# Factors of differences on GpSimd and ACT, units of two kinds in turn, experts chosen by sequence: a change to the last attention of an eight-layer kernel

## The chip, the core and the metric

The kernel runs on one core of one Trainium2 chip. The metric is the device time of one execution, in microseconds (us). The profile is one execution taken by the hardware profiler; its engines are PE (TensorE, matrix products), DVE (VectorE), ACT (ScalarE), POOL (GpSimd) and SP (the queue that starts most transfers). PE reads its operands from SBUF and writes into PSUM[...]. Each engine runs its instructions in the order in which they were queued, and waits for others by semaphores.

## The reference

The program is four pairs of an attention and a feed-forward, each followed by a residual sum and a layer norm, on x of 8 sequences, 256 positions and 256 features. Only the last pair is changed:

```python
# L3_attn: 16 heads of 16 features, each with two query/key pairs (a = 0, 1)
energy = einsum('bqhad,bkhad->bahqk', rope(q), rope(k)); causal mask
scores = softmax(energy / sqrt(16))
lam    = exp(sum(lq1*lk1)) - exp(sum(lq2*lk2)) + 0.2          # one per head
diff   = softmax(where(causal, NEG, scores[:, 0] - lam * scores[:, 1]))
att    = einsum('bhqv,bvhd->bqhd', diff, v); rms norm of each head; @ Wo
# L3_ffn: 32 experts, the 4 best of each token
probs  = softmax(x @ gate); w, idx = top_k(probs, 4); w = w / w.sum()
y      = sum over the 4 experts of w * ((u * silu(g)) @ down),  g, u = x @ gate_up
```

The softmax of a difference of two softmaxes is the heart of it: for each row, with e0 and e1 the exponentials of the two scores and s0, s1 their sums, the kernel forms e0 + c * e1 with c = -lam * s0 / s1 and scales it by r = 1 / s0. The ratio of the weights of the four experts does not depend on the sum over all 32.

## The kernel before, in words

Everything is one program written in a tile language; in the last attention and the last feed-forward the order of the instructions is written out by hand, and each engine keeps it.

**The attention (`attn3`).** The work is cut into 48 units, six for each sequence b. A unit has a half of the queries (qc) and some heads for four slots s: with qc = 0 it has two heads per slot and 128 keys (first kind: `Unit(b, 0, 0)` and `Unit(b, 0, 2)`), with qc = 1 one head and 256 keys (second kind: `Unit(b, 1, 0..3)`). Both kinds have the same number of scores, in four PSUM banks (tags "a" and "s", two buffers each); the first kind has sixteen exponentials of 128 elements, the second eight of 256. The order is by sequence, first the two units of the first kind, then the four of the second.

The loop over n at the end of `attn3` is a pipeline over units. Iteration n queues:
- `factors` of unit n-1: reciprocal r of the sums (L671, DVE), selection of the causal part of e0 with a fill (L676, POOL, two halves), c = s0 * r1 (L681) and c times minus lambda (L682), both POOL;
- `scores` of unit n: products (L641) and mask (L654) on PE, four negative maxima (L658, DVE), exponentials with their sums (L661, ACT);
- `values` of unit n-3: products with V (L738), and for the last head group a copy to oS (L118 or L120);
- a step of the projection of the next sequence (L595 on PE, evicted at L599 by DVE);
- the first half (slots 0 and 1) of `differences` of unit n-1: c * e1 + e0 (L695, DVE, one instruction for each slot and head), its negative maximum (L699, DVE), that times r (L700, POOL), and v = r * d + maximum (L703, POOL);
- one or two more steps of the projection, and a step of `finish` of an earlier sequence (L755 to L803: transposes, head norm, output product, residual, layer norm, and the transposed x for the feed-forward at L154);
- the second half of `differences`, then steps of the queue `others`;
- `turned` of unit n-2: v transposed by PE (L720) in two halves, each followed by an exponential on ACT (L722).

Projection, `finish`, `turned` and the gate products below all use PSUM banks of the tag "t", of which there are two.

**The experts (`ffn3_sort`, `place`, `scatter`).** The sequences form two groups of four. When x of sequence 3 is done, `others` gets the sort of group 0 for all eight tiles of 128 tokens at once: gate products (L1906), softmax over the experts without its sum (L1911 to L1916), the eight largest and their indices (L1921, L1922), then `place`: which expert has how many tokens (L893 to L902), where its tile begins, a slot for each token and expert (L907 to L926), and `tile_experts` (L935 to L944). Then 32 indirect transfers of POOL write the tokens to their slots in HBM (L953), three for each unit.

**The feed-forward (`ffn3`).** SP fetches the sorted rows in tiles (L1959) after the scatter is complete, then starts the loads of the down weights (L132). `ffn3_experts` goes over 63 tiles of group 0: transposes (L1970), products with gate and up (L1978), silu (L1985, ACT), product (L1987, DVE), transpose back (L1994), down (L2000), and a store. One small POOL copy per tile (L1990) marks the steps. Beside these tiles run what is left of `finish`, and then `ffn3_sort` for group 1. Then come the 63 tiles of group 1 with `ffn3_combine` of group 0 beside them (gathers L2045, weighted sums L2051), and at the end `ffn3_combine` of group 1.

Of the kernel before, what the change touches and what calls it, by code (L numbers as in the profile page):

```python
# [18 lines left out]
P = 128  # L19
# [20 lines left out]
class Model:  # L40


    def __init__(self, ctx, tc, ins, out):
# [23 lines left out]
        self.scattering = False  # L67
# [42 lines left out]
    def after(self, *call):  # L110

        self.left.append(call)

# [438 lines left out]
    def attn3(self, w, act, keep, start=False, beside=None):  # L552
# [4 lines left out]

        nc = self.nc
# [66 lines left out]
        class Unit:  # L625
# [41 lines left out]
            def factors(u):  # L667

                g = nc.gpsimd
                u.r = self.small.tile([P, 4, u.nh, 2], F32, tag="r3", name="r3")  # L670
                nc.vector.reciprocal(u.r, u.sums)  # L671
                u.c = self.small.tile([P, 4, u.nh], F32, tag="c3", name="c3")

                for i in range(2):
                    diag = u.e[:, 2 * i : 2 * i + 2, :, 0, u.nk - P :]
                    g.affine_select(  # L676
                        diag, diag, pattern=[[0, 2], [0, u.nh], [-1, P]],
                        compare_op=ALU.is_ge, fill=NEG, base=0, channel_multiplier=1,
                    )
                    if i == 0:  # L680
                        g.tensor_tensor(u.c, u.sums[:, :, :, 0], u.r[:, :, :, 1], ALU.mult)  # L681
                        g.tensor_tensor(  # L682
                            u.c, u.c, nlam[:, :, u.h0 : u.h0 + u.nh], ALU.mult
                        )

            def differences(u):
# [4 lines left out]
                for i in range(2):  # L691
                    two = slice(2 * i, 2 * i + 2)
                    for s in (2 * i, 2 * i + 1):
                        for h in range(u.nh):
                            nc.vector.scalar_tensor_tensor(  # L695
                                d[:, s, h, :], u.e[:, s, h, 1, :], u.c[:, s, h : h + 1],
                                d[:, s, h, :], ALU.mult, ALU.add,
                            )
                    nc.vector.tensor_reduce(nm[:, two], d[:, two], AX.X, ALU.max, negate=True)  # L699
                    nc.gpsimd.tensor_tensor(nm[:, two], nm[:, two], u.r[:, two, :, 0], ALU.mult)  # L700
                    for s in (2 * i, 2 * i + 1):
                        for h in range(u.nh):
                            nc.gpsimd.tensor_scalar(  # L703
                                u.v[:, s, h, :], d[:, s, h, :], u.r[:, s, h, 0:1],
                                nm[:, s, h : h + 1], ALU.mult, ALU.add,
                            )
                    yield
# [40 lines left out]
        def finish(b):  # L748
# [64 lines left out]
            if beside and b == GROUPS[0][1] - 1:  # L813
                others.append(beside(keep))
            yield

        others = []
        projections, ends, done = [], [], []

        def step(queue, n=1):  # L820

            while n and queue:
                if next(queue[0], StopIteration) is StopIteration:
                    queue.pop(0)
                else:
                    n -= 1

        for _ in project(0):
            pass
        units = [  # L830
            Unit(b, qc, h0) for b in range(NB) for qc in range(2) for h0 in range(0, 4, 2 - qc)
        ]
        for n in range(len(units) + 3):
# [11 lines left out]
            step(others)  # L845
# [11 lines left out]
            if not self.scattering:  # L857
                step(others, 2)
# [4 lines left out]
        return ends + others  # L863
# [1031 lines left out]
    def ffn3_sort(self, w, g, act, each=1):  # L1895


# [5 lines left out]
        lg = self.ps("t")[:, : n * 32].rearrange("p (t e) -> p t e", e=32)  # L1903
        for t in range(n):
            for c in range(2):
                nc.tensor.matmul(  # L1906
                    lg[:, t, :], self.xt(first + t // 2, t % 2, c), w["gate"][:, c, :],
                    start=(c == 0), stop=(c == 1),
                )
        nm = act.tile([P, n], F32, tag="r_nm", name="r_nm", bufs=1)  # L1910
        nc.vector.tensor_reduce(nm, lg, AX.X, ALU.max)  # L1911
        pr = act.tile([P, n, 32], F32, tag="r_pr", name="r_pr", bufs=1)
        nc.vector.tensor_tensor(
            pr, lg, nm.unsqueeze(2).to_broadcast([P, n, 32]), ALU.subtract
        )
        nc.scalar.activation(pr, pr, AF.Exp)  # L1916
        yield
        top = act.tile([P, n, 8], F32, tag="r_top", name="r_top", bufs=1)
        idx = act.tile([P, n, 8], U32, tag="r_idx", name="r_idx", bufs=1)
        for t in range(n):  # L1920
            nc.vector.max(top[:, t, :], pr[:, t, :])  # L1921
            nc.vector.max_index(idx[:, t, :], top[:, t, :], pr[:, t, :])  # L1922
            if t % 4 == 3 or t == n - 1:
                yield
        one, slots, ends = yield from self.place(w, act, self.const, f"f3{g}", idx[:, :, 0:4], n)
# [3 lines left out]
        next(rows)  # L1929
        expert = yield from self.tile_experts(w, act, self.const, f"f3{g}", ends)  # L1930

        wt = self.const.tile([P, n, 4], F32, tag=f"r_w{g}", name="r_w", bufs=1)
        sm = act.tile([P, n], F32, tag="r_sm", name="r_sm", bufs=1)
        nc.vector.tensor_reduce(sm, top[:, :, 0:4], AX.X, ALU.add)
        nc.vector.reciprocal(sm, sm)
        nc.vector.tensor_tensor(
            wt, top[:, :, 0:4], sm.unsqueeze(2).to_broadcast([P, n, 4]), ALU.mult
        )
        self.sorted[g] = wt, slots, expert
        self.scattering = True  # L1940
        yield
        for i, _ in enumerate(rows):
            if i % each == each - 1:
                yield
        self.scattering = False

    def ffn3_experts(self, w, g, act):
# [3 lines left out]
        rows, outs, expert, tiles = self.rows[g], self.outs[g], self.sorted[g][2], TILES[g]  # L1951
# [77 lines left out]
    def ffn3_combine(self, g, act, ahead):  # L2029
# [4 lines left out]
        wt, slots, _ = self.sorted[g]  # L2034
# [28 lines left out]
    def ffn3(self, w, act, left, start=False):  # L2063
# [3 lines left out]
        self.down = None  # L2067
        if start:
            for b in range(NB):
                self.transpose_x(b)  # L2070
            left = [self.ffn3_sort(w, 0, act)]
        if 0 not in self.sorted:
            for x in left:
                for _ in x:
                    pass
            left = []
        left = list(left) + [self.ffn3_sort(w, 1, act)]
        for j, _ in enumerate(self.ffn3_experts(w, 0, act)):

            if len(left) > 1 and j % 3 != 2:  # L2080
                continue
            while left and next(left[0], StopIteration) is StopIteration:
                left.pop(0)
        for x in left:
            for _ in x:
                pass
        put = self.ffn3_combine(0, act, 2)
# [6 lines left out]
        for _ in self.ffn3_combine(1, act, 1):  # L2094
            pass
# [3 lines left out]
def tile_layers(ctx: ExitStack, tc: tile.TileContext, ins, out, phases):  # L2099
# [26 lines left out]
    for i, name in enumerate(phases):  # L2126
        m.last = i == len(phases) - 1
        with tc.tile_pool(name=f"act{i}", bufs=2, side=sides[i % 2]) as act:
# [4 lines left out]
            with tc.manual_schedule(engines=engines) if name in MANUAL else ExitStack():  # L2133
# [20 lines left out]
                elif name == "attn3":  # L2154
                    beside = None
                    if not m.last:
                        beside = partial(m.ffn3_sort, stack[i + 1][1], 0, each=3)
                    left = m.attn3(w, act, kept[i], start=start, beside=beside)
                elif name == "ffn3":
                    m.ffn3(w, act, left, start=start)  # L2160
                    keeps[i - 1].close()
# [128 lines left out]
```

## Time and profile before

| what | us |
|---|---|
| median of three runs (2530.45 to 2537.91) | 2533.2 |
| the profiled execution's own time | 2531.46 |
| its span, from the first to the last instruction | 2529.7 |
| PE busy in the span | 2207.9 |
| DVE busy | 1431.1 |
| ACT busy | 1046.2 |
| POOL busy | 917.4 |
| last attention: first exponential to last | 1770.8 to 2225.5 |
| last feed-forward: first fetch of rows | 2226.92 |

Of each engine the profile counts the time in which an instruction is at work, not the time in which it waits. A share over the whole span says little here, since the eight layers have different limits; the stage between 1770 and 2226 us, and what follows it, has to be read by itself. In the timeline a row gives the start, the time it took, the engine, the line of the kernel and what was written and read; in brackets stands how long the engine had been idle before, and what ended that. Rows that follow each other without a gap are merged, so that "x2" means two instructions.

### The profile page before, as it was taken

Reading aid. Unit: us, or ns where it says so; the run is one execution under the profiler, and the core shown is the slowest. Engines: PE = TensorE matmul, PEld = TensorE weight load, DVE = VectorE, ACT = ScalarE, POOL = GpSimd, SP = SyncE. Lnnn points to the kernel's source line nnn. Section 1 sums busy time; section 2 is a strip of 40 time slices with the busy share of each in tenths; the row PEclk is TensorE's granted clock in tenths of the full one; section 3 lists DMA queues with packets and bytes.
Section 4 is the critical chain, followed back from the end, with each engine's and each line's share of the span. In section 5 each row is a group of like instructions: output and inputs, shape, how many; then the busy total and the mean of one; then the engine's idle time right before and its main releaser. Section 6 shows DMA issues by size and latency. Waiting matters only on the chain. (4 is left out here: it accounts for less than half of the span.)

```text
span 2529.7 us, 36310 instructions
## 1 busy us (share of the span) xinstructions
PE 2207.9 (87%) x12016; PEld 1497.5 (59%) x12016; DVE 1431.1 (57%) x3593; ACT 1046.2 (41%) x3005; POOL 917.4 (36%) x1725
## 2 busy tenths in 40 slices
PE   7999789899999999999999999998878777678990
PEld 4454588756666666666664465555555554467780
DVE  4555486754544544544465454565888888645363
ACT  1334355553544544534431112121766755634440
POOL 1222443343433323333312321000566647824445
PEclk9999999999999999999999999999989988789995
DMA  5000411100000100000250011002000000155663
GB/s 159 1 1 1 157 48 40 53 14 4 4 3 3 52 1 1 1 1 1 81 197 0 1 50 51 1 0 102 1 2 1 1 1 28 38 139 174 200 203 96
DMA packets 92309, 120.76 MB, mean 48 GB/s; under 512 B 9757, under 2 KB 79582, under 8 KB 91102
## 3 DMA queue, kind: packets, MB, share of 16 engines
q1 hardware_dynamic: 82270, 95.75, 11.8%
q0 software_dynamic: 8192, 21.11, 2.8%
q8 instruction: 100, 1.64, 0.3%
q10 hardware_dynamic: 1664, 1.57, 0.2%
q14 instruction: 83, 0.68, 0.1%
HBM read 67.53 MB, written 50.88 MB: 47 GB/s over the span
## 5 line engine op out<-in xcount | busy, mean ns | idle before, releaser
L1388 POOL TENSOR_SCALAR p<-p,rs 128x128 f32<-128x128 f32 (+1 forms) x256 | 104.6, 428 | 293.7 <-DVE rs L1386 289.4
L1378 ACT ACTIVATE p<-ps_s,nm,rq 128x128 f32<-128x128 f32 (+1 forms) x256 | 128.0, 507 | 151.0 <-DVE nm L1376 151.0
L1306 ACT ACTIVATE sq<-ps_a 128x512 f32<-128x512 f32 x126 | 76.0, 603 | 228.1 <-PE ps_a L1298 225.9
L146 POOL TENSOR_SCALAR rsq<-bnmv 128x2 f32<-128x2 f32 x64 | 13.6, 213 | 385.4 <-DVE bnmv L184 377.8
L661 ACT ACTIVATE e<-ps_a,nm 128x128 f32<-128x128 f32 (+1 forms) x256 | 105.9, 435 | 108.9 <-DVE nm L658 95.4
L1307 DVE TENSOR_REDUCE ssk<-sq 128x4 f32<-128x512 f32 x64 | 43.8, 686 | 172.6 <-ACT sq L1306 172.6
L703 POOL TENSOR_SCALAR v<-e,r,nmd 128x128 f32<-128x128 f32 (+1 forms) x256 | 134.9, 540 | 10.0
L1298 PE MATMUL ps_a<-w_a_wq,xT 128*128 128x512 f32 x256 | 123.2, 604 | 12.1 <-DVE k L1320 9.2
L1978 PE MATMUL ps_a<-w_f_gup,xTg 128*128 x504 | 113.1, 349 | 12.8 <-DVE xTg L1972 5.5
L720 PE MATMUL ps_t<-ident,v 128*128 128x128 f32 x384 | 67.8, 312 | 62.3 <-DVE qT L599 30.6
L1298 PE MATMUL ps_a<-w_a_wv,xT 128*128 128x512 f32 x256 | 120.5, 593 | 1.0 <-ACT q L1331 1.0
L695 DVE SCALAR_TENSOR_TENSOR e<-e,c 128x128 f32<-128x128 f32 (+1 forms) x256 | 105.6, 462 | 23.0 <-POOL c L682 22.8
L1307 DVE TENSOR_REDUCE ssq<-sq 128x4 f32<-128x512 f32 x64 | 43.9, 686 | 131.0 <-ACT sq L1306 131.0
L1298 PE MATMUL ps_a<-w_a_wk,xT 128*128 128x512 f32 x248 | 116.5, 593 | 0.0
L1426 PE MATMUL ps_o<-w_a_wo,attT 128*128 128x256 f32 x512 | 111.8, 379 | 0.0
L661 ACT ACTIVATE e<-ps_s,nm 128x128 f32<-128x128 f32 (+1 forms) x256 | 106.8, 451 | 0.0
L1426 PEld LDWEIGHTS ps_o<-w_a_wo,attT 128*128 128x128 f32 x512 | 96.7, 190 | 12.8
L1162 DVE SCALAR_TENSOR_TENSOR yg<-ps_t,xg,yg 128x128 f32<-128x128 f32 x266 | 93.1, 350 | 13.8 <-PE ps_t L1151 3.5
L1365 PE MATMUL ps_s<-kT,qT 128*128 128x256 f32 (+1 forms) x512 | 99.5, 327 | 0.0
L1978 PEld LDWEIGHTS ps_a<-w_f_gup,xTg 128*128 128x128 f32 x504 | 83.3, 199 | 25.2 <-issue 10.5
L720 PEld LDWEIGHTS ps_t<-ident,v 128*128 128x128 f32 x384 | 49.4, 160 | 81.8 <-POOL nmd L700 29.9
L1412 PE MATMUL ps_o<-pT,V 128*128 128x256 f32 x256 | 79.5, 392 | 19.3 <-ACT pT L120 19.3
(410 smaller groups left out, 6072.7 us busy)
## 6 DMA issues: line engine op xcount, KB each, us to landing
rows<-zero SPq DMA_DIRECT2D x42, 384.0 KB
xg<-rows SPq DMA_DIRECT2D x42, 384.0 KB
outs<-yg SPq DMA_DIRECT2D x42, 384.0 KB
w_f_gup<-in_f_gup SPq DMA_DIRECT2D x8, 768.0 KB
w_f_w<-in_f_w SPq DMA_DIRECT2D x8, 512.0 KB
w_f_down<-in_f_down SPq DMA_DIRECT2D x8, 384.0 KB
w_f_up<-in_f_up SPq DMA_DIRECT2D x5, 512.0 KB
lrows<-zero SPq DMA_DIRECT2D x12, 204.0 KB
```

Source lines behind the costliest of these rows:

```text
L661: nc.scalar.activation(e[:, s, j * nk : (j + 1) * nk], sc[s][:, j, :], AF.Exp, bias=nm[:, s, j : j + 1], scale=1.0, accum_out=sums[:, s, j ...
L695: nc.vector.scalar_tensor_tensor(d[:, s, h, :], u.e[:, s, h, 1, :], u.c[:, s, h : h + 1], d[:, s, h, :], ALU.mult, ALU.add,)
L703: nc.gpsimd.tensor_scalar(u.v[:, s, h, :], d[:, s, h, :], u.r[:, s, h, 0:1], nm[:, s, h : h + 1], ALU.mult, ALU.add,)
L720: nc.tensor.transpose(ps[:, s, c, :], x, self.ident)
L1162: nc.vector.scalar_tensor_tensor(acc[j], y, c, acc[j], ALU.mult, ALU.add)
L1298: nc.tensor.matmul(ps, self.xt(u.b, t, c), w[which][:, c, u.cols], start=(c == 0), stop=(c == 1),)
L1307: nc.vector.tensor_reduce(out, sq, AX.X, ALU.add)
L1365: nc.tensor.matmul(sc[:, j, :], u.qT[:, h0 + j, qc * P : (qc + 1) * P], u.kT[:, h0 + j, 0:nk], start=(j == 0), stop=False,)
L1378: nc.scalar.activation(u.p[qc][:, h0 + j, :], sc[:, j, :], AF.Exp, bias=nm[:, j : j + 1], scale=r[:, j : j + 1], accum_out=u.sums[qc][:, h ...
L1388: nc.gpsimd.tensor_scalar(u.p[qc][:, j, :], u.p[qc][:, j, :], ri[:, j : j + 1], 1.0, ALU.mult, ALU.mult,)
L1426: nc.tensor.matmul(y[:, t, :], attTs[b][:, h, t * P : (t + 1) * P], w["wo"][:, h, :], start=(h == 0), stop=(h == 15),)
L1978: nc.tensor.matmul(ps, xT[j][:, c, :], w["gup"][:, bass.ds(er[j], 1), c, :].rearrange("p o f -> p (o f)"), start=(c == 0), stop=(c == 1),)
```

## The change

It does three things in the last attention and one in what follows.

1. **Products and sums.** In `factors`, e1 is multiplied by c in place: in units of the first kind by one GpSimd instruction for all four slots and both heads (128x1024), in units of the second kind by four ACT instructions (128x256). In `differences`, VectorE only adds, one instruction for each half (128x512).
2. **Order of units.** In each sequence the order becomes first, second, second, first, second, second kind, in place of first, first, and four times second. The counts are the same.
3. **Choice of experts.** `ffn3_sort` and its use of `place` are cut into `ffn3_choose`, which is done for one sequence at a time when its x is done, `ffn3_place` for a group, and `ffn3_weights`, which is queued before the experts' tiles of group 0 and before the last combining of group 1. The choice goes by the largest logits, without an exponential; the weights of the four are computed later from the logits' differences to the largest. Sequences 0 to 6 are chosen with the attention's units, as far as these reach; sequence 7 and the placing of group 1 come in the feed-forward.
4. **Steps.** The transfers of the scatter are a queue of their own (`sends`), two for each unit; what is left of them is issued before the feed-forward's tiles. In the order of the built program, 28 of the 32 lie beside units, and four come after the last unit's v. The tiles of this stage now lie in the pool `keep`.

```diff
+                e1 = u.e[:, :, :, 1, :]
+                if u.qc == 0:
+                    g.tensor_tensor(
+                        e1, e1, u.c.unsqueeze(3).to_broadcast([P, 4, 2, P]), ALU.mult
+                    )
+                else:
+                    for s in range(4):
+                        nc.scalar.mul(e1[:, s, 0, :], e1[:, s, 0, :], u.c[:, s, :])
...
                 for i in range(2):
                     two = slice(2 * i, 2 * i + 2)
-                    for s in (2 * i, 2 * i + 1):
-                        for h in range(u.nh):
-                            nc.vector.scalar_tensor_tensor(
-                                d[:, s, h, :], u.e[:, s, h, 1, :], u.c[:, s, h : h + 1],
-                                d[:, s, h, :], ALU.mult, ALU.add,
-                            )
+                    nc.vector.tensor_tensor(d[:, two], u.e[:, two, :, 1, :], d[:, two], ALU.add)
...
-            if beside and b == GROUPS[0][1] - 1:
-                others.append(beside(keep))
+            if beside and b < NB - 1:
+                others.append(self.ffn3_choose(beside, keep, b))
+                if b == GROUPS[0][1] - 1:
+                    others.append(self.ffn3_place(beside, 0, keep, sends, each=2))
...
-        units = [
-            Unit(b, qc, h0) for b in range(NB) for qc in range(2) for h0 in range(0, 4, 2 - qc)
-        ]
+        order = ((0, 0), (1, 0), (1, 1), (0, 2), (1, 2), (1, 3))
+        units = [Unit(b, qc, h0) for b in range(NB) for qc, h0 in order]
...
-            step(others)
+            step(sends or others)
...
-            if not self.scattering:
-                step(others, 2)
+            step(others)
...
+    def ffn3_choose(self, w, keep, b):
...
+        ps = self.ps("t")[:, :64].rearrange("p (t e) -> p t e", t=2)
+        for t in range(2):
+            for c in range(2):
+                nc.tensor.matmul(
+                    ps[:, t, :], self.xt(b, t, c), w["gate"][:, c, :],
+                    start=(c == 0), stop=(c == 1),
+                )
+        lg = keep.tile([P, 2, 32], F32, tag="r_lg", name="r_lg", bufs=1)
+        nc.vector.tensor_copy(lg, ps)
+        yield
+        idx = keep.tile([P, 2, 8], U32, tag="r_idx", name="r_idx", bufs=1)
+        for t in range(2):
+            nc.vector.max(top[:, t0 + t, :], lg[:, t, :])
+            nc.vector.max_index(idx[:, t, :], top[:, t0 + t, :], lg[:, t, :])
...
+        ps = self.ps("t")[:, :128].rearrange("p (x t e) -> p x t e", x=2, t=2)
+        for x, m in ((0, self.ones), (1, self.behind)):
+            for k in range(4):
+                nc.tensor.matmul(
+                    ps[:, x], m, one[:, two, k, :],
+                    start=(x == 0 and k == 0), stop=(x == 1 and k == 3),
+                )
...
+        nc.vector.tensor_tensor(slot[:, two], ps[:, 1], upto[:, two], ALU.add)
+        yield
...
+    def ffn3_weights(self, g, keep):
...
+        nc.vector.tensor_tensor(
+            wt, top[:, :, 0:4], top[:, :, 0:1].to_broadcast([P, n, 4]), ALU.subtract
+        )
+        nc.scalar.activation(wt, wt, AF.Exp)
...
     def ffn3(self, w, act, keep, left, start=False):
...
+        def step(j):
+
+            if ends and j % 3 == 2:
+                self.step(ends)
+                if not ends:
+                    others.append(self.ffn3_choose(w, keep, last))
+                    others.append(self.ffn3_place(w, 1, keep, sends))
+            elif others:
+                self.step(others)
+            else:
+                self.step(sends)
+
+        wt = self.ffn3_weights(0, keep)
+        while sends:
+            self.step(sends)
         for j, _ in enumerate(self.ffn3_experts(w, 0, act)):
...
+            step(j)
```

`ffn3_place` has the second half of the former `place`, line for line, and then `tile_experts`, which is unchanged.

## The prediction

> **What bounds the kernel now.** I read four views in this order: the page, the busy time by stage, the waits, and the timeline of single engines inside the last attention.
>
> ```profile
> DVE  4555486754544544544465454565888888645363
> L703 POOL TENSOR_SCALAR v<-e,r,nmd 128x128 f32<-128x128 f32 (+1 forms) x256 | 134.9, 540 | 10.0
> L695 DVE SCALAR_TENSOR_TENSOR e<-e,c 128x128 f32<-128x128 f32 (+1 forms) x256 | 105.6, 462 | 23.0 <-POOL c L682 22.8
> ```
>
> The run of eights (slices of 63 us) is the last attention, 1770 to 2226 us: VectorE is the fullest engine there. L695 is what the change replaces.
>
> ```profile
> 1900.00:1950.00 50.00, 41.15 (x353) 28.70 (x352) 42.07 (x95) 34.91 (x136) 32.82 (x80) 0.90 0.01 1
> 2050.00:2100.00 50.00, 36.77 (x235) 26.09 (x236) 37.57 (x114) 19.54 (x62) 23.47 (x56) 0.67 0.01 4
> ```
>
> Columns: stretch, length, busy us of PE, PEld, DVE, ACT, POOL, clock, DMA. In the first stretch VectorE is busy 84%, ACT 70%, GpSimd 66%: full, but not saturated. In the second, the sort of the experts, every engine falls.
>
> ```profile
> 2038.53 0.21 POOL L681 TENSOR_TENSOR c<-sums,r 128x8 f32<-128x8 f32 x1
> 2112.54 0.21 POOL L681 TENSOR_TENSOR c<-sums,r 128x8 f32<-128x8 f32 x1
> 2171.17 0.21 POOL L681 TENSOR_TENSOR c<-sums,r 128x8 f32<-128x8 f32 x1
> ```
>
> L681 runs once per unit; these are the first units of sequences 5, 6 and 7. By the same row, sequences 1 to 4 take 53.9, 54.5, 52.8 and 53.2 us (mean 53.6). Sequence 5 takes 74.0 (the sort: 20.4 over the mean) and sequence 6 58.6 (its scatters: 5.0 over).
>
> ```profile
> 1892.45 0.19 DVE L671 RECIPROCAL r<-sums 128x8 f32<-128x8 f32 x1
> 1894.54 0.69 DVE L658 TENSOR_REDUCE nm<-ps_a 128x2 f32<-128x512 f32 x1 [1.89 <-PE ps_a L654]
> ...
> 1897.68 0.87 DVE L695 SCALAR_TENSOR_TENSOR e<-e,c 128x256 f32<-128x256 f32 x2
> 1898.59 0.69 DVE L699 TENSOR_REDUCE nmd<-e 128x2 f32<-128x512 f32 x1
> 1899.19 0.42 DVE L599 TENSOR_TENSOR qT<-ps_t,w_c_tq 128x256 f32<-128x256 f32 x1
> ...
> 1900.99 1.38 DVE L695 SCALAR_TENSOR_TENSOR e<-e,c 128x256 f32<-128x256 f32 x2
> ...
> 1903.01 0.19 DVE L671 RECIPROCAL r<-sums 128x8 f32<-128x8 f32 x1
> ```
>
> This is one unit. I read it as a ring between VectorE and PE: four maxima (2.4), an eviction (0.34), the first half of the differences (1.51, to 1899.19), evictions that free the two banks "t"; only then can PE turn the older unit (1.1 to 1.9), do the next scores (1.15) and mask (0.4); then the next maxima. From the freed banks to those maxima PE needs about 2.9 us, and the second half of the differences lies beside it. So of L695, the first half is on the ring and the second mostly not. The waits say the same: in 1800 to 2200 us PE's L720 waited 30.6 us for the eviction L599, and L658 17.3 us for PE's mask.
>
> [...]L164, 128x512 with one operand in PSUM, has 686. [...]the trace's exponentials of 128x256 with a pointer bias take 481 to 491 each[...]. [...]four L695 took 1.78 us beside L676 and 1.16 in another unit[...]. [...]GpSimd's 128x256 and 128x512 rows (L1612 732 ns, L1611 1326 ns) rise by 2.3 ns per element.
>
> **The change part by part.** The base is the profiled execution: 2531.5 us, of which 2529.7 span and 1.8 around it. The median of three is 2533.2, 1.7 above it, which I add at the end.
>
> 1. VectorE's product and sum becomes a sum: 256 instructions L695 (105.6 us busy) go, 96 adds of 128x512 come. From start to start such an instruction takes 0.60 (the maxima above do), so 57.6 us: VectorE gets 48 us freer. On the ring only the first halves count. Second kind (one head, 256 keys): 1.51 to 1.20, gain 0.31. First kind (two heads, 128 keys): 2.42 and 2.12 to the next instruction at 1878.66 and 1887.53, mean 2.27, to 1.20, gain 1.07. Per sequence 4 x 0.31 + 2 x 1.07 = 3.4; times 8, **-27**. Bounds: 0 and -48.
>
> 2. The products go elsewhere. In the 16 units of the first kind GpSimd gets one 128x1024 product: 1326 + 512 x 2.3 = 2.5 us, behind the second selection (0.64). In the 32 of the second kind ACT gets four of 128x256[...], queued ahead of the next unit's exponentials; behind them wait PE's scores, which need the exponentials' four banks. GpSimd: from a freed bank, 1.3 (second half) + 1.9 (v, selection to c) + 3.6 (c to product's end) = 6.8, against the ring's 2.9 + 2.4 + 0.34 = 5.7: late by 1.1. ACT: the products end at 1.3 + 1.9 + 0.6 + 1.7 = 5.5 where the exponentials began at 3.6. The eight exponentials of a second-kind unit (3.7 us) still end before PE asks; the sixteen of the first kind (5.6) are late by about 1.3. Both delays hit the same unit and overlap: 16 x 1.3 = **+21**. Bounds: 0 if PE's slow stretches hide it; in series, 16 x 3.1 and 32 x 0.9 give 78.
>
> 3. Taking turns (first, second, second) moves no work between engines; it only makes each long run of sixteen exponentials follow a unit with products on ACT, priced in 2. ACT's busy time per sequence becomes 37.4 + 16 x 0.4 = 44, under 53.6: 0.
>
> 4. The experts' choice by sequence replaces the burst. Gone: 20.4 + 5.0 + 3.7 (the last sequence's five intervals, 46.6 against a mean of 42.9) = 29. New: six choices inside attention (the seventh falls into the feed-forward). Each has gate products for two tiles (L1906: 3.65 us for eight, so 0.9) and an eviction that keeps a bank "t", then 2 us of small VectorE work, partly in the ring's gap: I take 2.5 each, bounds 0.9 and 4, so 15. The placing has about 6 us of VectorE in four pieces, of which 2.5 show. The scatters, two per unit instead of three: GpSimd's work per sequence today is 34.3 (in the trace a unit of the first kind holds it 5.9 us, 2176.2 to 2182.1, one of the second 4.05, 2158.95 to 2163.0; two and four of them, and 6.3 for L607, L767, L787 and the norms); with 2 x 2.5 and 12 x 1.27 it is 54.6 in the last two sequences. Today the same sum, 34.3 + 18 x 1.27 = 57.2, stands against 58.6 measured. I take 2.4 over the mean each, so 5. Sum 22.5 - 29 = **-7**; bounds -20 and +6.
>
> 5. Four scatters are left when the last unit's v is done. Today the rows are fetched 2.0 us after it (2226.92), held by the last values. New: 4 x 1.27 + 2.7 (landing, as the last gather shows) = 7.8. All of SP's queue, the down weights too, stands behind that fetch: **+6**; bounds 3 and 7.
>
> 6. In the feed-forward the second group's sort shrinks to one choice and the placing, with no exponential and so no two table loads (1.28 each). From 2274 to 2298 us the tiles (L1990, one each; usual step 1.6) lose 5.3 + 1.4 + 3.1 + 1.9 = 11.7; I leave 3.7: **-8**; bounds -11 and -3. The weights move ahead of each combining: some 2.5 us, beside the first four gathers (1.25 each).
>
> Sum -27 + 21 - 7 + 6 - 8 = -15: 2516.5, and with 1.7 **2518 us**.
>
> **The rivals.**
> - VectorE's share is the bound, so all of step 1 comes out and step 2 is hidden: -48 - 9 = -57, 2476. For it: 84% busy. Against it: its idle time is waits for PE.
> - The attention doesn't move: steps 1 and 2 cancel, -9 remains: 2524. For it: the waits of PE on "t" are not touched.
> - The factors' chain is the bound: slower. One mechanism, at L681/L682: from c to the next c runs a chain GpSimd, ACT, VectorE, GpSimd. Today its pure length is 5.71 (second kind, 1861.27 to 1866.98) and 7.4 (first). After: 5.85 (0.6 to the factor, 0.9 for two products on ACT, 2.5 for two adds and two maxima, 1.9 for v, selection and c) and 8.55 (0.4, 3.1 for selection and product, 2.5, 2.55), so per sequence 4 x 0.14 + 2 x 1.15 = 2.9 more; if all that today lies over the chain stays, +23 in eight, and -9: +14, 2547. It decides when c and products come later than the 2.8 us of maxima and eviction that cover it; today VectorE waits for c 13 times, 13.7 us.
>
> **How the numbers follow.** Forecast 42%, own range 2503 to 2530; VectorE's share 16%; no move 18%; chain 24%. Steps 1 and 2 are large terms of opposite sign, so the range reaches to 2487 and 2548, leaving out 2 in 10. A measurement can tell about 0.3% (7.6 us) from no change. Faster by more: 0.36 + 0.16 + 0.09 = 0.61. Within: 0.06 + 0.07 + 0.03 = 0.16. Slower: 0.02 + 0.21 = 0.23.
>
> **What would show it.** Step 1: adds near 0.69 us, VectorE under 80% in the attention. Step 2: the products near 2.5 and 0.49 us, exponentials waiting for products, VectorE waiting for GpSimd's product. The steady sequences at 53 to 54 us. Step 4: no sequence over 60. Step 5: a fetch released by the scatter, 7 to 8 us after the last v. Step 6: no table load between 2260 and 2300. It is wrong if steady sequences take under 50 or over 56 us.

## The result and the profile after

| | before | after |
|---|---|---|
| median of five runs, us | 2534.9 (2530.5 to 2537.9) | 2614.2 (2613.2 to 2620.8) |
| span of the profiled execution | 2529.7 | 2611.9 |
| first to last c of the attention | 440.9 | 521.5 |
| last c to the end of the span | 312.0 | 314.0 |
| VectorE, ACT, GpSimd busy in the span | 1431, 1046, 917 | 1402, 1095, 953 |

The ratio is 1.0320, interval 1.0307 to 1.0332: 79 us slower, where 15 us faster was forecast. Nearly all of it lies in the attention: 80.6 us between the first c and the last (c is the factor -lam * s0 / s1, made once for each unit).

First the page of the kernel after: VectorE's row of slices (65 us each), and its group of sums.

```profile
DVE  4655486654454444454564445466665666535363
L710 DVE TENSOR_TENSOR e<-e 128x512 f32<-128x512 f32 x96 | 69.1, 719 | 53.3 <-ACT e L701 33.3
```

The eights of the attention have become sixes. VectorE's work has shrunk as intended, 105.6 us to 69.1, but it now stands idle 53 us in front of these sums (23.0 in front of L695 before), most of it for ACT's products (L701). The busy time by stage, same stretches as before:

```profile
1900.00:1950.00 50.00, 31.94 (x255) 21.74 (x256) 32.61 (x71) 30.04 (x106) 30.44 (x71) 0.80 0.00 1
2050.00:2100.00 50.00, 34.45 (x270) 23.68 (x272) 29.10 (x66) 35.31 (x137) 25.72 (x58) 0.80 0.00 1
```

In the first stretch no engine is full: VectorE 65%, ACT 60%, GpSimd 61%, PE 64% at a clock of 0.80. When every engine has become emptier and the time longer, they wait for each other. The second stretch, where the sort was before, now looks like the first. The rows of c for the first units of sequences 4, 5 and 6 (counted from 0):

```profile
2036.76 0.20 POOL L690 TENSOR_TENSOR c<-sums,r 128x8 f32<-128x8 f32 x1
2105.12 0.21 POOL L690 TENSOR_TENSOR c<-sums,r 128x8 f32<-128x8 f32 x1
2176.85 0.20 POOL L690 TENSOR_TENSOR c<-sums,r 128x8 f32<-128x8 f32 x1
```

The sequences take 55.0, 65.3, 68.4, 71.6, 68.4, 71.7 and 66.9 us (before: 47.2, 53.9, 54.5, 52.8, 53.2, 74.0, 58.6). The burst of the sort is gone from sequence 5, the sixth number, but every other sequence is 8 to 19 us longer.

Now one loss, in the timeline of the kernel after (engines mixed; in brackets how long the engine had been idle, and for whom):

```profile
2004.85 2.24 POOL L715 TENSOR_SCALAR v<-e,r,nmd 128x128 f32<-128x128 f32 x4
...
2006.11 0.69 DVE L711 TENSOR_REDUCE nmd<-e 128x4 f32<-128x512 f32 x1
...
2006.71 0.19 DVE L680 RECIPROCAL r<-sums 128x8 f32<-128x8 f32 x1
...
2007.67 1.28 ACT L792 ACT_TABLE_LOAD   x1
...
2009.10 1.07 ACT L734 ACTIVATE p<-ps_t 128x512 f32<-128x512 f32 x2
2009.34 0.25 POOL L793 TENSOR_TENSOR ms<-ms,rr 128x32 f32<-128x32 f32 x1 [1.95 <-ACT rr L792]
...
2010.05 0.68 DVE L667 TENSOR_REDUCE nm<-ps_s 128x2 f32<-128x512 f32 x1
...
2010.65 1.20 POOL L799 TENSOR_TENSOR att<-att,rr 128x256 f32<-128x256 f32 x2
...
2012.12 1.74 POOL L715 TENSOR_SCALAR v<-e,r,nmd 128x128 f32<-128x128 f32 x4
...
2014.20 0.20 POOL L690 TENSOR_TENSOR c<-sums,r 128x4 f32<-128x4 f32 x1
...
2014.72 1.70 ACT L701 ACTIVATE e<-e,c 128x256 f32<-128x256 f32 x4 [4.55 <-POOL c L691]
...
2016.33 0.45 ACT L670 ACTIVATE e<-ps_a,nm 128x256 f32<-128x256 f32 x1
...
2019.92 0.61 ACT L810 COPY aT<-ps_t 128x512 f32<-128x512 f32 x1
...
2020.67 0.66 PE L732 MATMUL ps_t<-ident,v 128*128 128x128 f32 x2 [7.75 <-ACT aT L810]
...
2020.69 0.20 POOL L690 TENSOR_TENSOR c<-sums,r 128x4 f32<-128x4 f32 x1
```

The reciprocal is ready at 2006.90; c needs two small GpSimd instructions more. But GpSimd's queue has other work ahead: v of the older unit, the head norm of `finish` (which itself waits for ACT's table load), att, the second half of v, a selection. So c comes at 2014.69, 7.8 us after r. ACT has been idle since 2010.17, in front of products that need c. Behind them stand eight exponentials whose maxima were ready at 2010.73; they begin at 2016.33. Behind these stand the copy aT and the exponential p, which would free the banks "t"; so PE's turn of the older unit waits 7.75 us, and with it the next scores. In this trace ACT kept to the order of its queue: exponentials whose operands were there did not pass four products that waited, and began 5.6 us late (2010.73 to 2016.33). In 1800 to 2200 us of the list of waits:

```profile
ACT e L701 <- POOL c L691: 53.4, 14, 5.3
...
PE ps_t L732 <- ACT aT L810: 31.0, 4, 7.7
```

Before, that place in ACT's queue didn't exist: VectorE waited for c itself, 13.7 us in the same stretch. The delay of c on GpSimd did exist. Here is a c in the kernel before that stood behind the head norm:

```profile
1855.67 0.19 DVE L671 RECIPROCAL r<-sums 128x8 f32<-128x8 f32 x1
...
1857.06 0.25 POOL L781 TENSOR_TENSOR ms<-ms,rr 128x32 f32<-128x32 f32 x1 [1.95 <-ACT rr L780]
...
1861.27 0.21 POOL L681 TENSOR_TENSOR c<-sums,r 128x4 f32<-128x4 f32 x1
...
1861.38 0.64 ACT L798 COPY aT<-ps_t 128x512 f32<-128x512 f32 x1
```

It comes at 1861.76, 5.9 us after its r. But ACT had by then done the next unit's exponentials and was copying aT: nothing on ACT waited for it.

At the end of the attention (timeline; SPq is SP's queue):

```profile
2307.02 1.29 POOL L715 TENSOR_SCALAR v<-e,r,nmd 128x256 f32<-128x256 f32 x2
...
2312.39 0.96 POOL L959 DMA_INDIRECT rows<-X,r_slots  x1 [0.30 <-issue]
2316.38 0.92 SPq L2043 DMA_DIRECT2D xg<-rows  x2
```

From the last v to the fetch it is 8.1 us (2308.31 to 2316.38), as the forecast's step 5 had it (7.8).

### The profile page after: what moved, and what is told of

Same layout as the page of the kernel before. It is cut to its first block, busy times and chain, and to the rows that moved or that the text cites. A ratio compares the mean times of both kernels' runs of the same rounds, so it can differ in the third digit from the quotient of the medians.

```text
span 2611.9 us, 36409 instructions
## 1 busy us (share of the span) xinstructions
PE 2216.6 (85%) x12008; PEld 1500.5 (57%) x12064; DVE 1402.1 (54%) x3457; ACT 1094.5 (42%) x3132; POOL 952.8 (36%) x1739
## 5 line engine op out<-in xcount | busy, mean ns | idle before, releaser
L2062 PE MATMUL ps_a<-w_f_gup,xTg 128*128 x504 | 110.9, 344 | 14.4 <-DVE xTg L2056 6.0
L667 DVE TENSOR_REDUCE nm<-ps_a 128x2 f32<-128x512 f32 (+1 forms) x96 | 65.4, 681 | 75.1 <-remote 44.4
L1432 PEld LDWEIGHTS ps_o<-w_a_wo,attT 128*128 128x128 f32 x512 | 96.7, 190 | 12.8
L1168 DVE SCALAR_TENSOR_TENSOR yg<-ps_t,xg,yg 128x128 f32<-128x128 f32 x266 | 93.1, 350 | 13.7 <-PE ps_t L1157 3.3
L710 DVE TENSOR_TENSOR e<-e 128x512 f32<-128x512 f32 x96 | 69.1, 719 | 53.3 <-ACT e L701 33.3
```

Of the source, the lines that this page charges most:

```text
L1168: nc.vector.scalar_tensor_tensor(acc[j], y, c, acc[j], ALU.mult, ALU.add)
L1432: nc.tensor.matmul(y[:, t, :], attTs[b][:, h, t * P : (t + 1) * P], w["wo"][:, h, :], start=(h == 0), stop=(h == 15),)
L2062: nc.tensor.matmul(ps, xT[j][:, c, :], w["gup"][:, bass.ds(er[j], 1), c, :].rearrange("p o f -> p (o f)"), start=(c == 0), stop=(c == 1),)
```

## The experiments

Theory A: ACT's queue was tied to GpSimd's by products that stand ahead of the exponentials and wait for c. Rivals: B, the order of the units; C, the choice by sequence (its gate products take banks "t"); D, GpSimd's own product. Ratios are to the kernel before on the same chip (its median there was 2522 to 2535 us), with 95% intervals; 0.1% is 2.5 us.

**The three parts alone.** e1 has the products and sums, on the kernel before (in the code, `e1` is a tile, the exponentials of the second score, and not this run):

```diff
+                e1 = u.e[:, :, :, 1, :]
...
+                        nc.scalar.mul(e1[:, s, 0, :], e1[:, s, 0, :], u.c[:, s, :])
...
-                            nc.vector.scalar_tensor_tensor(
...
+                    nc.vector.tensor_tensor(d[:, two], u.e[:, two, :, 1, :], d[:, two], ALU.add)
```

> The kernel before with step 2 and the sums of step 1 alone (products on GpSimd and ACT, VectorE adds); units in the old order, experts chosen in the old burst. Theory A (ACT's queue: the second-kind products stand there ahead of the next unit's exponentials and wait for GpSimd's factors): most of the 79 us is here, 2590 to 2615 us, intervals of second-kind units of 14 us and more. In the old order four second-kind units follow each other, so under A each of these is late. Theory B (the order of the units costs it): 2500 to 2540. Theory C (the choice by sequence costs it): 2500 to 2540.

e2 has the order alone:

```diff
-        units = [
-            Unit(b, qc, h0) for b in range(NB) for qc in range(2) for h0 in range(0, 4, 2 - qc)
-        ]
+        order = ((0, 0), (1, 0), (1, 1), (0, 2), (1, 2), (1, 3))
+        units = [Unit(b, qc, h0) for b in range(NB) for qc, h0 in order]
```

> The kernel before with step 3 alone: first- and second-kind units take turns. A: within 10 us of the kernel before (2525 to 2545). B: 2570 to 2610. C: within 10 us.

e3 has the choice by sequence, the placing and the queue of scatters alone:

```diff
-                others.append(beside(keep))
+                others.append(self.ffn3_choose(beside, keep, b))
...
+                    others.append(self.ffn3_place(beside, 0, keep, sends, each=2))
...
```

> The kernel before with steps 4 to 6 alone: experts chosen by sequence, placed in steps, scatters beside the units. A: the forecast's own terms for these steps, -7, +6 and -8, so 2520 to 2535, and no sequence over 60 us. C: 2570 to 2610, with every sequence from the second on longer than 58 us. B: 2520 to 2540.

e4 is the kernel after with the sums and products of e1 undone:

> The kernel after without the products: order of the units and choice by sequence, VectorE multiplies and adds as in the kernel before. A: 2515 to 2540, the loss gone. B or C alone: 2570 to 2615. If the loss needs the products together with one of the others, this is fast too, and the kernel with products alone as well.

| kernel | products | order | choice | ratio |
|---|---|---|---|---|
| e1 | new | old | old | 1.0268 (1.0247 to 1.0290) |
| e2 | old | new | old | 1.0026 (1.0015 to 1.0038) |
| e3 | old | old | new | 0.9969 (0.9960 to 0.9979) |
| e4 | old | new | new | 1.0016 (1.0006 to 1.0026) |
| after | new | new | new | 1.0320 (1.0307 to 1.0332) |

B and C fall: the products carry the loss. Choosing by sequence gains 0.31% (8 us), and the order costs 0.26% alone and 0.47% on top of the choice (7 to 12 us). In e3 no sequence took over 58.2 us. The total of e1 came as A had it, its shape did not. I had expected 14 us and more at each second-kind unit. In e1's sequences 2 to 4 the steps to the four second-kind units took 9.3 to 9.4, 8.3 to 8.8, 13.3 to 13.8 and 6.5 us (before: 7.7 to 8.0, 8.8 to 9.9, 10.8 to 11.4 and 5.7), and the largest loss was in the step from the sequence before, 15.5 to 16.4 (10.2 to 11.0). With old order, e12 joins products and choice:

> The kernel after with the old order of the units (products and choice by sequence stay). If the three parts add: products 67, choice -8, so 2580 to 2590. If the choice's matmuls and evictions on the banks t collide with the late products: 2595 to 2615.

It gave 1.0261 (1.0235 to 1.0286), 2599 us and so in the upper of my two ranges, where e1 and e3 add up to 1.0237; that lies inside the interval, so whether the two disturb each other stays open.

**Which product.** e5 keeps ACT's products and gives the first kind back to VectorE:

```diff
-                if u.qc == 0:
-                    g.tensor_tensor(
...
-                else:
+                if u.qc:
                     for s in range(4):
...
```

> The kernel after, but units of the first kind have VectorE's product and sum as before; units of the second kind keep ACT's four products. Theory A (ACT's queue: products that wait for GpSimd's factors stand ahead of the next unit's exponentials): most of the loss stays, 2580 to 2610 us. Theory D (GpSimd's product of a first-kind unit lengthens the way from c to the sums): 2525 to 2545.

e6 keeps GpSimd's product and gives the second kind back to VectorE:

```diff
-                else:
-                    for s in range(4):
-                        nc.scalar.mul(e1[:, s, 0, :], e1[:, s, 0, :], u.c[:, s, :])
...
```

> The kernel after, but units of the second kind have VectorE's product and sum as before; units of the first kind keep GpSimd's product and VectorE's sum. A: 2505 to 2535, the loss gone. D: 2570 to 2600.

e5 gave 1.0252 (1.0235 to 1.0269), e6 1.0067 (1.0050 to 1.0084): over e4, ACT's products cost 2.4% (60 us) and GpSimd's 0.5% (13 us). With 2540 us e6 lies above the range that A had. D holds for the small part: in e6 the c after a first-kind unit comes 10.3 us after that unit's c where e4 has 8.5, which is the 1.9 us of the product. e11 puts all 48 products on GpSimd:

```diff
-                if u.qc == 0:
...
-                        e1, e1, u.c.unsqueeze(3).to_broadcast([P, 4, 2, P]), ALU.mult
...
+                    e1, e1, u.c.unsqueeze(3).to_broadcast([P, 4, u.nh, u.nk]), ALU.mult
```

> The kernel after with all products on GpSimd (one of 128x1024 in each of the 48 units, 1.9 us as in the kernel after), none on ACT. A: faster than the kernel after, as ACT waits for GpSimd no more; by the interval that GpSimd's product adds (1.8 us per unit that follows such a product, at most 48 x 1.8 = 86 over e10) 2545 to 2590. D alone (GpSimd's product in the chain of factors is worth more than ACT's queue): 2600 or more.

It gave 1.0259 (1.0240 to 1.0277), 2598 us: 0.6% better than after, as A has it, but above the range that I gave. VectorE then waited 59.7 us for GpSimd's products in 1800 to 2200 us. GpSimd is no free place for them either.

**Place, duration or wait.** e7 queues ACT's products behind the next unit's exponentials:

```diff
...
             if u:
                 u.scores()
+            if last:
+                last.products()
```

> The kernel after with ACT's products of a second-kind unit queued behind the next unit's exponentials instead of ahead of them: same work, another place in ACT's queue. A: half of the loss or more is gone, 2520 to 2570; the sums come later, but the exponentials don't wait for GpSimd any more. D: 2600 to 2625, no change, or slower, since the sums wait for 3.6 to 5.6 us of exponentials.

It gave 1.0469 (1.0451 to 1.0486): worse. This half of A was wrong: I had counted on ACT's wait going (it did, 53 us to 3.6 in 1800 to 2200 us), and overlooked who stands behind the sums. From the waits of e7, 1800 to 2200 us:

```profile
DVE e L714 <- ACT e L705: 75.9, 23, 4.5
```

VectorE's queue now stands in front of its sum while ACT does up to sixteen exponentials (5.6 us, as from 1770.80 to 1776.41 in the kernel before), and behind that sum stand the evictions that free banks "t". The wait had moved from ACT's queue to VectorE's (VectorE's wait for ACT's products was 20.0 us in the kernel after). e8 makes every product one key column wide; it leaves the other columns unmultiplied, so e8, and e10 after it, compute other weights than the reference:

```diff
-                e1 = u.e[:, :, :, 1, :]
+                e1 = u.e[:, :, :, 1, 0:1]
...
```

> The kernel after with every product taken over one key column instead of all (the other columns are left unmultiplied, so that the weights are not those of the reference): the instructions, their places in the queues and their waits for c stay, their duration goes. A1 (the wait for c in ACT's queue costs it, not the 1.7 us of products): 2570 to 2600 us. A2 (the duration of the products costs it): 2495 to 2530.

e10 does so too, with all products on GpSimd and none on ACT:

```diff
-                else:
-                    for s in range(4):
-                        nc.scalar.mul(e1[:, s, 0, :], e1[:, s, 0, :], u.c[:, s, :])
+                e1 = u.e[:, :, :, 1, 0:1]
+                g.tensor_tensor(e1, e1, u.c.unsqueeze(3), ALU.mult)
```

> The kernel after with the products of all units replaced by a product over one key column on GpSimd (the other columns are left unmultiplied, so that the weights are not those of the reference); ACT has none. The sums on VectorE and their wait for c stay. This is step 1 with step 2 taken out, over the kernel without products (e4, 1.0016). Forecast's step 1: 27 us less than that, 2500. If VectorE's time was not the bound: 2520 to 2535. Theory A lets both stand; a time above 2545 would be against it.

e8 gave 1.0170 (1.0154 to 1.0187), e10 0.9973 (0.9965 to 0.9980). With ACT's four instructions in its queue, however short, 2.0% (50 us) are lost; their length and that of GpSimd's products make another 1.5% (38 us; over sequences 2 to 4 the intervals behind GpSimd's product, 2 and 5 of the table below, have 2.7 of 4.6 us a sequence). Then the wait by itself. e15 is e4 (VectorE multiplies and adds) with four more products by c on ACT, at the place of the kernel after, into a spare tile that nobody reads; e16, not shown, has a constant column in place of c:

```diff
+                if u.qc == 1:
+                    x = act.tile([P, P * 2], F32, tag="dum", name="dum", bufs=1)
+                    for s in range(4):
+                        nc.scalar.mul(x, u.e[:, s, 0, 1, :], u.c[:, s, :])
```

> The kernel after without products (e4, 1.0016), with four additional products by c per second-kind unit on ACT, at the place that they have in the kernel after, into a spare tile that nothing reads. VectorE multiplies and adds by itself. A1 (wait for c): 1.018 to 1.030. If the loss comes from the sums waiting for ACT: 1.002 to 1.010.

> As the last, but the factor is a constant (a column of the unit matrix), so that ACT waits for nobody: only its 1.7 us per second-kind unit stay. A1: 1.003 to 1.012. If ACT's occupied time costs it: 1.018 to 1.030, the same as by c.

e15 gave 1.0297 (1.0281 to 1.0313), e16 1.0042 (1.0026 to 1.0057). Same instructions, same place, same length; the wait alone is 2.55%, 65 us. The groups by form show it, e15 and then e16 (busy, mean ns | idle before, for whom):

```profile
L697 ACT ACTIVATE dum<-e,c 128x256 f32<-128x256 f32 x128 | 65.0, 508 | 77.3 <-POOL c L691 74.2
```

```profile
L698 ACT ACTIVATE dum<-e,ident 128x256 f32<-128x256 f32 x128 | 64.9, 507 | 3.1
```

In e15 the sums don't wait for ACT. So it isn't the late sums that cost most, but what stands behind the products on ACT. The intervals from c to c (us) say where, by the place of the unit in its sequence, over sequences 2 to 4; the first is the step from the sequence before, and the fourth reaches the second unit of the first kind:

| kernel | 1 | 2 | 3 | 4 | 5 | 6 |
|---|---|---|---|---|---|---|
| e4 | 10.2 to 12.2 | 8.5 | 6.3 to 6.9 | 13.3 to 14.0 | 12.8 | 5.7 |
| e16 | 13.0 to 13.6 | 8.5 | 6.1 to 6.9 | 12.8 to 14.4 | 12.8 | 5.7 |
| e15 | 16.3 to 17.1 | 8.5 | 6.6 to 9.2 | 13.5 to 15.9 | 12.8 | 6.6 |
| after | 16.0 to 16.1 | 10.3 | 7.0 to 8.8 | 14.1 to 15.9 | 14.1 | 6.5 |

e15 shows the kernel after in all the units that follow one of the second kind (1, 3, 4, 6); the rest, 2 and 5, is GpSimd's product. The traces of both also say which products wait. In each of these sequences ACT stands idle for c twice, 4.0 to 4.7 us each: at the products of the second and of the fifth unit, which are the second-kind units right behind one of the first kind. The other two second-kind units find their c ready. So the two intervals behind each wait carry the loss: over e16, e15 loses 2.5 us a sequence in 3 and 4, and 4.4 in 6 and 1.

e13 leaves all products in place and makes c on VectorE right behind the reciprocal, so that no GpSimd instruction stands on the way to c:

```diff
+                nc.vector.tensor_tensor(u.c, u.sums[:, :, :, 0], u.r[:, :, :, 1], ALU.mult)
+                nc.vector.tensor_tensor(u.c, u.c, nlam[:, :, u.h0 : u.h0 + u.nh], ALU.mult)
...
-                        g.tensor_tensor(u.c, u.sums[:, :, :, 0], u.r[:, :, :, 1], ALU.mult)
-                        g.tensor_tensor(
-                            u.c, u.c, nlam[:, :, u.h0 : u.h0 + u.nh], ALU.mult
-                        )
```

> The kernel after with the two small multiplications that make c moved from GpSimd to VectorE, right behind the reciprocal: c no longer stands behind v and a selection on GpSimd. Theory A1 (ACT's wait for GpSimd's c): ratio to the kernel before falls from 1.032 to 1.010 to 1.020, and ACT's waits for c (53 us in 400) to under 15. If the duration and the place of the products alone cost it: 1.027 to 1.035.

It gave 1.0041 (1.0026 to 1.0057): two instructions moved, 2.8% (71 us) of the 3.2% gone, more than I had said. Groups by form of ACT's products, after and then e13:

```profile
L701 ACT ACTIVATE e<-e,c 128x256 f32<-128x256 f32 x128 | 54.5, 498 | 71.9 <-POOL c L691 71.9
```

```profile
L698 ACT ACTIVATE e<-e,c 128x256 f32<-128x256 f32 x128 | 54.4, 498 | 12.1 <-DVE c L683 11.9
```

The same work at the same speed, and 60 us less idle time ahead of it. e9 asked for the share of one bank, by copying aT on VectorE:

```diff
-            nc.scalar.copy(aT, pt)
+            nc.vector.tensor_copy(aT, pt)
```

> The kernel after with one copy a sequence moved from ACT to VectorE: aT, which frees a bank t and which in the kernel after stands behind products and exponentials, with PE's turns of an older unit waiting for the bank up to 7.7 us. Theory A with the bank as its second half (the wait for c reaches PE through that bank): the first interval of each sequence falls from 16 to 11 to 13 us, so 20 to 35 us less, 2580 to 2594. If the late scores have another cause: 2605 to 2620.

It gave 1.0278 (1.0256 to 1.0299), 11 us better than after and half of what I expected: the first interval fell only to 14.2 to 15.0. aT is one of the things behind the products, not the main one.

**A faster version.** e14 takes c to VectorE in the kernel with the choice alone:

> The kernel with the choice by sequence alone (old order, no products: 0.9969) with the same move of c to VectorE. VectorE waited 13.7 us for c and spends 96 x 0.2 = 19 us on it: A says 0.990 to 1.000.

e17 has the choice, the old order, ACT's products for the second kind with c made on VectorE, and VectorE's product and sum for the first kind; e18 copies aT on VectorE as well:

```diff
+                if u.qc:
+                    nc.vector.tensor_tensor(u.c, u.sums[:, :, :, 0], u.r[:, :, :, 1], ALU.mult)
...
-                    if i == 0:
+                    if i == 0 and u.qc == 0:
...
+                    for s in (2 * i, 2 * i + 1) if u.qc == 0 else ():
...
```

> Choice by sequence, old order; in units of the second kind c is made on VectorE, ACT multiplies and VectorE adds; in units of the first kind c is made on GpSimd and VectorE multiplies and adds, as before. If products on ACT pay once they don't wait for GpSimd: under 0.9969, the kernel with the choice alone, some 0.985 to 0.995. If ACT's 1.7 us a unit take back what VectorE's sums save (e16: 0.26% over e4): 0.995 to 1.003.

> The same with aT copied on VectorE instead of ACT. If aT's place behind ACT's exponentials still holds PE: 0.2 to 0.4% less than the last. If VectorE is the fuller engine again: the same or slower.

e14 gave 0.9985 (0.9978 to 0.9992), e17 1.0022 (1.0009 to 1.0034), e18 1.0014 (1.0005 to 1.0022). None beats e3. That e18 is not clear of e17 goes with the second of my two expectations for it: aT's place on ACT no longer costs anything that shows. Even without the wait, products on ACT don't pay here: e17's steady sequences take 58 to 61 us where e3 has 56 to 57.5. The best version is e3: the change's third part without the first two, 0.9969.

## Why the prediction was wrong

The sum, term by term. The runs telescope: before to e3, e4, e10 and after.

| step | forecast, us | runs | measured, us |
|---|---|---|---|
| 1, VectorE only adds | -27 (0 to -48) | e10 over e4 | -11 |
| 2, products on GpSimd and ACT | +21 (0 to 78) | after over e10 | +88 |
| 3, taking turns | 0 | e4 over e3 | +12 |
| 4 to 6, choice, left-over scatters, sort in the feed-forward | -9 | e3 | -8 |

These are differences of ratios. From the first to the last c, in one profile each, the same four steps are -6, +86, +7 and -6 us: the large term is sure, the terms of steps 1 and 3 to some 5 us only.

**The step that failed is step 2**, in this sentence: "ACT: the products end at 1.3 + 1.9 + 0.6 + 1.7 = 5.5 where the exponentials began at 3.6." Its 0.6 and 1.7 held: the rows above have 0.52 us from c to the products (2014.20 to 2014.72) and 1.70 for the four, and over all units a product took 0.498 in the mean, with 0.40 from start to start. The 1.9, "v, selection to c", was read from a unit where nothing else stood on GpSimd. In the rows shown above c comes 7.9 us after the second half's maximum (2006.80 to 2014.69), since the queue also holds the first half of v and the head norm, once a sequence. The profile before had this already, in sequences 1 to 4 5.9 us from r to c at the head norm and 2.2 to 3.2 at the other units; no exponentials stood behind it there. I wrote down the wait and who stood behind it (exponentials, then scores), but costed it as a fixed delay, and asked only whether the exponentials of one unit come late. Two things were left out. Behind the exponentials stand p and the copies that free the banks "t", so PE's turns and scores are late too; how much of the loss goes that way was not separated, since e9 took only one such copy off ACT (11 us). And c of the next unit needs the sums that these exponentials give: from c over products, exponentials, reciprocal to the next c is a ring. The rows above show it closed once: c at 2014.69, products to 2016.42, exponentials, the next c from 2020.69 on. A delay in it isn't hidden. Products that wait for nobody cost 7 us in all (e16 over e4, 2.1 us a unit); those that wait cost 65 us more. "Late by about 1.3" per first-kind unit, 16 times, was the size; the measured 88 us are even above the upper bound of 78, worked out from lengths alone.

**The slower rival** had the right direction and the wrong ring, so its sign is no proof of its mechanism. It ran c, product, sums, v, selection, c, without the exponentials, and gave 5.85 us for the second kind and 14 us in all. The shortest second-kind interval measured is 6.5 us (before 5.7), but most of the loss lies in the units where GpSimd or PE is late, which a pure length doesn't show.

**Step 1** had the right durations (0.72 us measured, 0.69 forecast) and the wrong worth. e10 keeps the sums with products of 0.2 us and gains 11 us over e4, though VectorE has some 33 us less work there. The groups by form, e4 (the wider of two forms; both together have 101.5 us) and then e10:

```profile
L704 DVE SCALAR_TENSOR_TENSOR e<-e,c 128x256 f32<-128x256 f32 x128 | 60.8, 515 | 21.4 <-POOL c L691 21.3
L704 DVE TENSOR_TENSOR e<-e 128x512 f32<-128x512 f32 x96 | 68.3, 712 | 34.2 <-POOL e L695 34.1
```

Of the 33 us, 13 went into waiting longer for GpSimd in front of the sums, 34 in place of 21. So 84% busy was no sign that the path would get shorter by what is taken off.

**Step 3** was put at 0; it costs 7 us alone (e2; 3 of them from the first to the last c) and 12 with the choice (e4 over e3). In e4 interval 4 is 13 to 14 us where e2 has 9.5; that is the interval in which the choice's work lies. Why the order costs 7 us by itself wasn't traced further. It also makes two second-kind units a sequence follow one of the first kind, and these are the two whose products wait; but in the old order the products lose nearly as much (e12 over e3 2.9%, after over e4 3.0%).

**Steps 4 to 6** held, in sum and one by one. In the kernel after the stretch from the last v to the fetch grew from 2.0 to 8.1 us (forecast +6), and from the fetch to the end it fell from 302.8 to 295.5 (forecast -8; between e1 or e2 and e3 or e4, all on one chip, it fell by 10). From the first to the last c e3 is 6 us shorter than before (forecast -7). A choice costs 3.4 us in e3 (57.4, 56.1 and 57.1 us in sequences 2 to 4, against 54.5, 52.8 and 53.2), where 2.5 was forecast; sequences with placing and scatters take 58.2 and 56.3, in place of 74.0 and 58.6. The two table loads that the sort caused in the feed-forward (for L1916 and back to silu, 1.28 us each) are gone; the weights of group 1 have one, at 2552.60 (L2024, 1.28 us).

Of the signs that I named, these came: adds near 0.69 (0.72 in the mean), products near 0.49 (0.498), VectorE under 80% (58 to 72% in 1800 to 2200 us, by stretches of 50 us), the fetch 8 us after the last v (8.1). GpSimd's product took 1.90 us in place of 2.5, and six of the seven sequences took over 60. The one that I called decisive came on the wrong side: steady sequences over 56 us.

What stays open: the granted clock of PE in this stage lay at 0.80 to 0.88 after (1800 to 2250 us, by stretches of 50 us; 0.86 to 0.99 before, outside the sort and the last scatters), and PE's work took longer: a score product of 32x256 507 ns in the mean against 469, one of 32x128 419 against 341. From before to after both PE's busy share and the clock fell: in 1900 to 1950 us the share went from 82% to 64% and the clock from 0.90 to 0.80. Stretch by stretch the two don't go together: before, the stretch from 1950 to 2000 had a share of 74% and the highest clock, 0.99. What sets the clock is not shown here. How many of the 88 us pass through these longer products was not separated: no kernel here changes the clock alone.

## What to carry to other kernels

Before work goes to a less busy engine, ask what stands behind it in that engine's queue and for whom it waits: in the kernel after, ACT's products that waited for GpSimd held all that followed in the queue, also what was ready (eight exponentials, 5.6 us). Here four short products cost 7 us when they waited for nobody, and 65 us more when they waited for GpSimd; moving the two instructions that made their operand took nearly all of the loss back. The late operand was there before the change, where it cost little; look in the profile before for the latest arrival of what the moved work will need, not for a typical one. A busy share of 84% says how much work there is, not how much of it lies on the path.

## What the hardware showed beyond that

GpSimd's product of 128x1024 with the factor spread over 128 keys took 1.90 us. The forecast's 2.5 was extended from L1611 and L1612, two-input additions with both inputs at full width; whether the spread factor makes the difference wasn't tried. Four ACT products of 128x256 into four places took 1.70 us; into one and the same spare tile (e15, e16) 2.12 us, whose cause wasn't tried. VectorE's sum took 0.719 us in the mean, but not evenly: 88 of the 96 took 0.67 to 0.71 us, and five took 1.20. These five began while GpSimd's two-input L616 (0.72 us) had just started (0.07 to 0.08 us before). One more sum, at 1781.09, had started 0.16 us before L616; it took its 0.68, and L616 took 1.10. So in these six pairs the later of the two took longer, by some 0.5 and 0.4 us. The prediction's example of L695 beside L676 is less clean than it says: beside the four L695 that took 1.78 us ran L607 too (1879.01 to 1879.77), another two-input instruction of GpSimd, and not L676 alone.
